# Four-layer graph kernel: layer 1's newest quarter last, weighing beside the scores, elu in PSUM, degrees in bfloat16 column tiles

## The chip, the cores and the metric

One core of one Trainium2 chip. The metric is the device time of one execution in microseconds (us). The kernel before took 1742.03 us (median of three runs, 1739.12 to 1742.09).

## What is computed

x has 8 batches of 2048 nodes with 64 features, adj is a 2048 x 2048 matrix of zeros and ones with a full diagonal, and H says which nodes belong to which of 64 hyperedges. Four layers follow each other, and each is `x = layernorm(x + layer(x))`. Cut to what the change touches:

```python
# layer 0: per node n and each hyperedge e that holds it
all_he = elu(beta[b,e,n] * h[b,n] + (1 - beta[b,e,n]) * agg[b,e])
g = sum_e coefs1[b,n,e] * all_he[b,e,n]
industry = (adj / deg) @ (x @ W_ind)          # deg = row sums of adj
c = softmax(attn_scores([industry, g]))       # tanh(f @ fcW + fcb) @ av
x = layernorm(x + c[0] * industry + c[1] * g)
# layer 1
dinv = rsqrt(row sums of (adj + I))
x = layernorm(x + (dinv * ((adj + I) @ (dinv * x))) @ W.T)
# layer 2: products with adj, apt = softmax(relu(emb @ emb.T)), node-wise weights, a bias
# layer 3: three steps of v = relu([v, adj @ v] @ W1.T + b1) @ W2.T + b2
```

## The kernel before, in words

adj (transposed) lies in SBUF for most of the kernel, in 16 row blocks of 128 and two column halves (`adj`, `adj_more`). The batches are handled as four pairs, so that 2 x 64 features fill 128 partitions or columns; the nodes as four quarters of 512, each of four tiles of 128. A product of adj with a pair takes float32r operands in two parts (high and low, `split`, L168), so each output quarter takes 2 x 16 matmuls of 128x512, and a pair 128 of them. The trace calls them `ug` (layer 0, `products`) and `u` (later layers). All matmuls go through `mm` (L172) and all transposes through `transpose` (L175); both keep the order of the program, which is thus the order of TensorE. `pin`, `hold` and `kept` are short names for the same fixing on other engines. What isn't fixed is put in order by a scheduler that goes by readiness and the program's order.

Stages, with their times in the profile: a start (h, the sums of agg, the nodes' rows gathered by hyperedge), to about 62 us. The **attention** of layer 0, to about 222 us: 16 node tiles, sorted so that the first has 12 steps and the last 1 or 2, 57 steps in all. In a step three matmuls put h and agg of one hyperedge slot into a PSUM tile `pz` (a ring of three, shared with small transposes), VectorE multiplies by the ratio `R` (L793), ScalarE takes exp (L795), VectorE makes elu by max and min (L797, into SBUF as `y`) and weighs it by `co` (L800 for a tile's first step, L802 for the others), and GpSimd adds it to `acc` (L803). At a tile's end GpSimd stores `acc` by an indirect DMA (L805). At a tile's first step `begin` prepares the next tile: GpSimd's gather, the split of its rows, sixteen-column matmuls `ps`, and four small VectorE instructions for `R` and `co` (L761 to L767). `slots` (L288 to L300) prepares the one-hot matrices of the tile after next, mostly on ScalarE.

**Mixing** of layer 0 and **layer 1** run together, to about 512 us. Mixing has 16 steps, one per pair and quarter: `mix_ind` (product with W_ind, scaling by the degree), `mix_g` (load and transpose of g), `mix_scores` (four tanh), `mix_weigh` (`pd`, a sigmoid as tanh, L937), `mix_end` (transposes `pt`, sum, layernorm, store to x1 in HBM). What TensorE does between them comes from a filler: a generator that gives one matmul of 128x512 at a time, first the rest of layer 0's products, then layer 1. `fill(n)` takes n of them. `tick`, `after` and `later` count filler matmuls and start other work when so many have gone by, so delays are written in matmuls. In attention, too, `fill(5)` and `fill(3)` are taken at each step, 345 in all. When layer 1 needs a part of x1 that isn't there, its generator answers "wait" and no matmul is put in.

The degrees come from 64 matmuls of float32r with a matrix of ones (`du`, in `degrees`), taken from the same filler between the first pair's two halves; `inverses` then makes 1/degree and dinv on VectorE and GpSimd.

Layer 1 takes each pair's parts from x1 (`l1_parts`), scales and splits them, makes its products in two halves of 128 x 512 x 2 columns, and `l1_end` multiplies by W, adds and normalizes. After mixing, `make_el` prepares the embeddings of layer 2 (`pb`, the bias), and `load_xn` loads pairs 0 to 2 of layer 1's result back, on ScalarE's DMA queue. Then apt (first score product `s` at 512.5 us), layer 2 and layer 3 follow.

Of the kernel before, what the change touches and what calls it, by code (L numbers as in the profile page):

```python
# [56 lines left out]
def tile_gnn_fast(  # L57
# [164 lines left out]
    ones_r = hy.tile([P, P], F32R, name="ones_r")  # L222
    nc.vector.tensor_copy(ones_r, ones)
# [118 lines left out]
    def products():  # L342
# [3 lines left out]
        def degrees(g):  # L346
            du = pph.tile([P, 2, C], F32, tag="ph", name=f"du{g}", bufs=2)
            for t in range(NT):
                for i in range(2):
                    mm(  # L350
                        du[:, i, :], lhsT=ones_r, rhs=adj_c(t, 2 * g + i), start=t == 0, stop=t == NT - 1
                    )
                    yield
            for i in range(2):
                c = 2 * g + i
                r = slice(c * P // NCH, (c + 1) * P // NCH)
                evacuate(deg4[r, :], du[r, i, :])

        def inverses():

            pdc = places["small"]([P, JT, P], "pdc")
            for j in range(JT):
                transpose(pdc[:, j, :], deg4[:, cols(j, P)])
            pdc = pdc.rearrange("p j (c r) -> p c j r", c=NCH)[:, :, :, 0]
            d1 = deg1.rearrange("p (c j) -> p c j", c=NCH)
            nc.vector.tensor_scalar(d1, pdc, 1.0, None, op0=ALU.add)
            nc.gpsimd.tensor_tensor(dinv, deg1, neg_half[:, :NT], ALU.pow)
            nc.vector.tensor_scalar(d1, pdc, 1.0, None, op0=ALU.max)
            nc.vector.reciprocal(deg1, deg1)
            for _ in range(20):  # L370
                yield
            for c in range(NCH):
                pt = places["small"]([P, C], "pinv")
                for j in range(JT):
                    k = c * JT + j
                    transpose(pt[:, cols(j, P)], deg1[:, k:k + 1].to_broadcast([P, P]))
                row = va.tile([P, C], F32, tag="ut", name="inv", bufs=2)
                nc.scalar.copy(row, pt)
                nc.sync.dma_start(inv_hbm[:, cols(c)], row)
                for _ in range(4):  # L380
                    yield

        for p in range(NP):
            for g in range(2):
# [3 lines left out]
                turning = inverses() if p == 0 and g == 1 else iter(())  # L388
                for t in range(NT):
                    for i in range(2):  # L390
                        for c in own:
                            mm(
                                u[c], lhsT=part[t // JT][i][:, t % JT, :], rhs=adj_c(t, c),
                                start=t == 0 and i == 0, stop=t == NT - 1 and i == 1,
                            )
                            tick()
                            if t > 1:
                                next(turning, None)
                            yield
                    if p == NP - 1 and g == 1 and t % JT == JT - 1:  # L400
                        first_parts(t // JT, free)
                    if p + 1 < NP and t % JT == JT - 1:
                        c = t // JT
                        if g == 1:
                            parts(p + 1, c)
                        if g == 1 and c < 2 or g == 0 and c >= 2:
                            fetch(p + 1, (c + 2) % NCH)
# [8 lines left out]
                if p == 0 and g == 0:  # L416
                    yield from degrees(0)
                    yield from degrees(1)
# [323 lines left out]
    with ExitStack() as pb_scope:  # L742
# [3 lines left out]

        def begin(t):
# [9 lines left out]
            for s, o in enumerate(ohs):  # L757
# [3 lines left out]
            nc.vector.tensor_tensor(  # L761
                R[:, 0:S], ps[:, 0:S, 0, :], hrow[:, None, BF:BF + 8].to_broadcast([P, S, B]), ALU.add
            )
            nc.vector.tensor_reduce(R[:, S], ps[:, 0:S, 1, :].rearrange("p s b -> p b s"), AX.X, ALU.add)
            nc.vector.reciprocal(R[:, 0:S + 1], R[:, 0:S + 1])
            co = pl.tile([P, 12, B], F32, tag="co", name="co", bufs=2)
            nc.vector.tensor_tensor(  # L767
                co[:, 0:S], ps[:, 0:S, 1, :], R[:, S:S + 1, :].to_broadcast([P, S, B]), ALU.mult
            )
            return S, both, ohs, R, co  # L770
# [3 lines left out]
        now = begin(0)  # L774
        slots(tiles[1], pps, "mm", 3)
        for k, t in enumerate(tiles):
            S, both, ohs, R, co = now
            acc = pl.tile([P, B, F], F32, tag="acc", name="acc", bufs=2)
            for s in range(S):
# [13 lines left out]
                nc.vector.tensor_tensor(z, z, R[:, s, :, None].to_broadcast([P, B, F]), ALU.mult)  # L793
                y = pl.tile([P, B, F], F32, tag="y", name="y", bufs=3)
                nc.scalar.activation(y, z, AF.Exp, bias=-1.0)  # L795

                nc.vector.scalar_tensor_tensor(y, z, 1.0, y, op0=ALU.max, op1=ALU.min)  # L797
                cb = co[:, s, :, None].to_broadcast([P, B, F])
                if s == 0:
                    nc.vector.tensor_tensor(acc, y, cb, ALU.mult)  # L800
                else:
                    nc.vector.tensor_tensor(y, y, cb, ALU.mult)  # L802
                    nc.gpsimd.tensor_tensor(acc, acc, y, ALU.add)  # L803

            nc.gpsimd.indirect_dma_start(  # L805
                out=gs_hbm[:], out_offset=bass.IndirectOffsetOnAxis(ap=order[:, t:t + 1], axis=0),
                in_=acc.rearrange("p b f -> p (b f)"), in_offset=None,
            )
# [97 lines left out]
    def mix_scores(i):  # L906
# [17 lines left out]
        after(5, differences)  # L924
        r, gn = rs[i], gns.pop(i)
# [37 lines left out]
    def l1_parts(p, c):  # L963
# [4 lines left out]
        y = staged("y")  # L968
        nc.sync.dma_start(y, x1_hbm[p][:, wide(c), :])

        def scale():
            pin(nc.gpsimd.tensor_tensor(y, y, dinv[:, wide(c), None].to_broadcast([P, JT, P]), ALU.mult))

        def cast():
            part[p, c] = split(va, y, f"v{c}", 1, [P, JT, P], pin=True)

        after(16, scale, 6, cast)

    def l1_load(p, c):
        x1 = staged("x1")  # L980
        nc.sync.dma_start(x1, x1_hbm[p][:, wide(c), :])
        return x1

    def l1_end(p, c, ut, x1):
# [5 lines left out]
        def add_up():  # L990
            pin(nc.vector.tensor_tensor(r, po, dinv[:, wide(c), None].to_broadcast([P, JT, P]), ALU.mult))
            pin(nc.gpsimd.tensor_tensor(r, r, x1, ALU.add))

# [7 lines left out]
        after(4, add_up, 6, *normalized(lp, r, dst, True, end))  # L1001
# [10 lines left out]
    def layer1(p):  # L1012

        for g in range(2):
            own = (2 * g, 2 * g + 1)
            ug = None
            for t in range(NT):
                while (p, t // JT) not in part:
                    yield "wait"
                if ug is None:  # L1020
                    ug = pph.tile([P, 2, C], F32, tag="ph", name="u1", bufs=2)
                    u = {c: ug[:, c % 2, :] for c in own}
                for i in range(2):
                    for c in own:
                        mm(
                            u[c], lhsT=part[p, t // JT][i][:, t % JT, :], rhs=adj_c(t, c),
                            start=t == 0 and i == 0, stop=t == NT - 1 and i == 1,
                        )
                        tick()
                        yield  # L1030
                if g == 1 and p + 1 < NP and t % JT == JT - 1:
                    l1_parts(p + 1, t // JT)
            for k, c in enumerate(own):
                ut = va.tile([P, C], F32, tag="ut", name="ut", bufs=2)
                pin(nc.scalar.copy(ut, u[c]))
                later(6 + 8 * k, lambda p=p, c=c, ut=ut, x1=l1_load(p, c): l1_end(p, c, ut, x1))
# [18 lines left out]
    for i in range(steps + 1):  # L1055
        k = 9 if i > NCH else 8
        if i < steps:
            mix_scores(i)
            fill(k)
        if i > 0:  # L1060
            mix_end(i - 1)
            fill(k)
        if i + 1 < steps:
# [3 lines left out]
            fill(k)  # L1067
        if i < steps:
            mix_weigh(i)
# [49 lines left out]
    fill(32)  # L1119
    for c in range(NCH):  # L1120
        make_el(c)
        fill(16)
        if c == 1:

            room.append(True)
            load_xn()
    norms = staged("emb").rearrange("p t f -> p (t f)")[:, 0:NT * D].rearrange("p (t d) -> p t d", d=D)
    nc.sync.dma_start(norms, emb.rearrange("(t p) d -> p t d", p=P))
    nc.vector.tensor_tensor(norms, norms, norms, ALU.mult)
    nrm = ap_.tile([P, NT], F32, name="nrm")  # L1130
    nc.vector.tensor_reduce(nrm, norms, AX.X, ALU.add)
    nc.vector.tensor_reduce(wrong[:, 5:6], nrm, AX.X, ALU.max)
    nc.vector.tensor_scalar(wrong[:, 5:6], wrong[:, 5:6], SUM_LIMIT, None, op0=ALU.is_gt)
# [590 lines left out]
    def check():  # L1724
        t, k = checks.pop(0)
        ar = va.tile([P, C], F32R, tag="ut", name="ar", bufs=2)
        nc.scalar.copy(ar, seen_a)  # L1727
        nc.vector.scalar_tensor_tensor(  # L1728
            ar.bitcast(F32), seen_a, 1.0, ar.bitcast(F32), op0=ALU.mult, op1=ALU.not_equal,
            accum_out=left[:, t, k:k + 1],  # L1730
# [892 lines left out]
```

## Time and profile before

| what | value |
|---|---|
| median of three runs | 1742.03 us (1739.12 to 1742.09) |
| profiled execution | 1745.85 us |
| its span | 1743.7 us |
| mean granted TensorE clock | 0.984 |
| busy: PE, DVE, ACT, POOL | 95%, 48%, 34%, 33% of the span |
| last exponential of attention starts | 221.4 us |
| last `pt` of mixing starts | 460.2 us |
| first `pb` starts | 481.2 us |
| first `s` of layer 2 starts | 512.5 us |

How it is read: a page gives for each engine the busy time in the span, and for groups of equal instructions the source line, the tiles that they write and read, their number, their busy time in us, the mean duration of one in ns, and the idle time of the engine ahead of them with what ended it. PE is TensorE's matmuls, PEld its weight loads, DVE VectorE, ACT ScalarE, POOL GpSimd, SP the queue that issues most transfers. In a list of waits, "A x L1 <- B y L2: 11.1, 12, 2.5" says that engine A sat idle ahead of line L1 for 11.1 us in 12 times, the longest 2.5 us, until engine B had done line L2. A table by stages gives for each stretch of time its length and each engine's busy time with the number of instructions.

### The profile page before, as it was taken

The numbers are of one execution on the slowest core, as the hardware profiler recorded it, in microseconds if no ns is written. First come the engines' busy times: TensorE is split into PE (matmuls) and PEld (weight loads), VectorE is DVE, ScalarE is ACT, GpSimd is POOL, SyncE is SP. The second block draws the span as 40 slices with busy tenths as digits, with TensorE's granted clock in tenths as the row PEclk, the third lists the DMA queues.
The fourth block names the chain that finished last, engine by engine and source line by source line (L and its number), as shares of the span: only waits on it lengthen the run. The fifth ranks groups of instructions, "written<-read, shape, count | busy, mean of one in ns | idle before, by whom it ended". The sixth has DMA issues, their size and how long they took to land.

```text
span 1743.7 us, 27994 instructions
## 1 busy us (share of the span) xinstructions
PE 1660.8 (95%) x11196; PEld 1209.8 (69%) x11196; DVE 832.2 (48%) x1547; ACT 589.5 (34%) x1031; POOL 571.8 (33%) x515
## 2 busy tenths in 40 slices
PE   6888899999899999999999999999989999999996
PEld 4667666666674444478788878888767877878775
DVE  7688845778642221210136147777523433433332
ACT  1345533444222212111213267878512222212221
POOL 4578845556534443422023001313210200202001
PEclk9999999999999999999999999999999999999998
DMA  9833334444330000027344457675571121211211
GB/s 342 277 126 124 125 122 136 142 145 146 112 121 6 30 27 5 24 71 293 112 133 138 117 137 154 138 168 123 152 260 43 49 61 43 61 48 42 57 42 39
DMA packets 171180, 195.83 MB, mean 112 GB/s; under 512 B 71536, under 2 KB 116336, under 8 KB 169760
## 3 DMA queue, kind: packets, MB, share of 16 engines
q1 hardware_dynamic: 160096, 154.54, 30.4%
q0 software_dynamic: 8544, 30.68, 5.2%
q10 hardware_dynamic: 2400, 8.72, 1.4%
q8 instruction: 90, 1.47, 0.4%
q14 instruction: 50, 0.41, 0.1%
HBM read 126.72 MB, written 67.17 MB: 111 GB/s over the span
## 4 chain that ended last, share of the span: by engine, by line
PE 78%; DVE 4%; DMA 3%; POOL 2%; issue 2%; ACT 1%; SPq 1%; POOLq 0%; ACTq 0%; DVEq 0%
PE u L172 39%; PE ua L172 13%; PE py L172 8%; PE pw L172 6%; PE ug L172 3%; PE pr L172 2%; PE po L172 1%; PE pf L172 1%; PE pt L175 1%; PE s L172 1%; PE pd L172 1%; PE pi L172 1%; PE pz L172 1%; POOL ln_r L862 0%; DMA adj_more<-adj_hbm 0%
## 5 line engine op out<-in xcount | busy, mean ns | idle before, releaser
L172 PE MATMUL ua<-pt,xn 128*128 128x512 f32 x512 | 230.2, 592 | 1.4 <-DVE pt L1150 1.4
L172 PEld LDWEIGHTS ua<-pt,xn 128*128 128x128 f32 x512 | 96.9, 190 | 111.1 <-issue 104.0
L1514 DVE COPY w_half<-pw 128x512 f32<-128x512 f32 x160 | 109.7, 705 | 91.1 <-PE pw L172 90.2
L1510 ACT COPY w_half<-pw 128x1024 f32<-128x1024 f32 x128 | 130.0, 1015 | 61.6 <-PE pw L172 61.5
L172 PE MATMUL py<-w_half,xg 128*32 128x128 f32 x4096 | 144.2, 281 | 3.2 <-issue 3.2
L172 PE MATMUL u<-adj,v0h 128*128 128x512 f32 x384 | 134.4, 427 | 1.1 <-ACT h L1818 1.1
L172 PEld LDWEIGHTS py<-w_half,xg 128*32 128x32 f32 x4096 | 112.5, 138 | 21.3 <-issue 4.6
L172 PE MATMUL u<-adj_more,v2h 128*128 128x512 f32 x384 | 126.5, 408 | 0.0
L172 PE MATMUL u<-adj_more,v2l 128*128 128x512 f32 x384 | 124.6, 401 | 0.0
L172 PE MATMUL u<-adj,v0l 128*128 128x512 f32 x384 | 124.5, 402 | 0.0
L172 PE MATMUL pw<-est,wst 64*128 64x256 f32 x1024 | 110.8, 320 | 0.8 <-ACT w_half L1510 0.4
L1156 POOL TENSOR_TENSOR acc<-acc,pt 128x512 f32<-128x512 f32 x60 | 76.5, 1276 | 104.2 <-DVE pt L1150 103.5
L1150 DVE TENSOR_SCALAR pt<-pt 128x512 f32<-128x512 f32 x64 | 29.8, 465 | 152.4 <-ACT pt L1149 152.3
L172 PEld LDWEIGHTS pw<-est,wst 64*128 64x128 f32 x1024 | 82.7, 187 | 26.3 <-ACT w_half L1510 16.7
L1727 ACT CAST ar<-fcav 128x512 fp32r<-128x512 f32 x64 | 39.5, 618 | 169.2 <-DMA fcav<-in_adj_t 164.5
L172 PE MATMUL u<-adj_more,v3l 128*128 128x512 f32 x288 | 93.8, 401 | 2.0 <-DVE v3l L168 2.0
L1728 DVE SCALAR_TENSOR_TENSOR ar<-fcav,ar 128x512 f32<-128x512 f32 x64 | 45.2, 707 | 102.9 <-ACT ar L1727 102.9
L172 PE MATMUL u<-adj,v1h 128*128 128x512 f32 x288 | 93.7, 403 | 0.0
L1149 ACT ACTIVATE pt<-s 128x512 f32<-128x512 f32 x64 | 38.0, 598 | 164.4 <-PE s L172 164.4
L172 PE MATMUL u<-adj_more,v3h 128*128 128x512 f32 x288 | 93.6, 403 | 0.0
L1699 POOL TENSOR_TENSOR x<-x,rows 128x512 f32<-128x512 f32 x16 | 22.6, 1433 | 212.0 <-PE pt L175 127.7
L172 PE MATMUL u<-adj,v1l 128*128 128x512 f32 x288 | 92.0, 397 | 0.0
(406 smaller groups left out, 3273.2 us busy)
## 6 DMA issues: line engine op xcount, KB each, us to landing
fcav<-in_adj_t SPq DMA_DIRECT2D x64, 256.0 KB, 2.9
u_hbm<-ut SPq DMA_DIRECT2D x48, 256.0 KB, 2.8
xg<-u_hbm SPq DMA_DIRECT2D x24, 512.0 KB, 7.1
adj<-in_adj_t POOLq DMA_DIRECT2D x16, 512.0 KB, 7.7
adj_more<-in_adj_t POOLq DMA_DIRECT2D x16, 512.0 KB, 7.4
adj_hbm<-adj_more SPq DMA_DIRECT2D x16, 512.0 KB, 6.1
x_hbm<-r SPq DMA_DIRECT2D x28, 256.0 KB, 2.4
hs_hbm<-st ACTq DMA_DIRECT2D x8, 584.0 KB, 5.9
```

The source lines that it names most:

```text
L172: tc.keep_in_program_order(nc.tensor.matmul(*args, **kw))
L175: tc.keep_in_program_order(nc.tensor.transpose(dst, src, ident))
L1149: nc.scalar.activation(pt, s, AF.Exp)
L1150: nc.vector.tensor_scalar(pt, pt, 1.0, None, op0=ALU.max)
L1156: nc.gpsimd.tensor_tensor(accs[c], accs[c], pt, ALU.add)
L1510: pin(nc.scalar.copy(dst, pw.rearrange("p j o n -> p n (j o)")))
L1514: pin(copy(dst[:, :, 2 * j:2 * j + 2], bank.rearrange("p o n -> p n o")))
L1699: nc.gpsimd.tensor_tensor(xs, xs, b2.to_broadcast([P, JT, P]), ALU.add)
L1727: nc.scalar.copy(ar, seen_a)
L1728: nc.vector.scalar_tensor_tensor(ar.bitcast(F32), seen_a, 1.0, ar.bitcast(F32), op0=ALU.mult, op1=ALU.not_equal, accum_out=left[:, t, k:k ...
```

## The change

- *Degrees.* The upper halves of adj's float32 words are read as bfloat16 (adj holds only zeros and ones), with a stride of two. 64 matmuls of 128x32 by 128x512 in four column tiles sum one quarter each; they come in four bursts of 16 inside the second half of pair 0's product (at row blocks 5, 9, 13, 15) and are not taken as filler slots. One copy takes the result out. `inverses` runs in the next pair's first half, with longer distances.
- *Attention.* elu is written back into PSUM, and the weighing reads it there. It is issued one step later: mult(s), weigh(s-1), elu(s), in this fixed order. The four ratio instructions for the next tile follow the first elu of the tile. The exponential gets its own tile in `y`'s ring of three.
- *Mixing.* `mix_weigh` and `mix_end` of a step move into the next step's round: weigh beside the next scores, the end one fill later. The sum of x and g moves from the scores to `mix_sum`. Fills are 11 or 12, three a round, instead of 8 or 9, four a round.
- *Layer 1.* Both halves of a pair are begun before its newest quarter is needed; the quarters that a half takes are 0, 1, 2 and later 3, the other 0, 1 and later 2, 3. Staging tiles are given out through a queue (`ask`, `serve`, `left`).
- *After mixing.* `load_xn` comes ahead of `fill(40)` (before: after the second `make_el`, which followed `fill(32)`), the distances of `make_el` are 12 instead of 16, and the check of the embeddings' norms goes through the queue.
- *Layer 3.* The check of the input compares a bfloat16 copy.

```diff
-        def degrees(g):
-            du = pph.tile([P, 2, C], F32, tag="ph", name=f"du{g}", bufs=2)
-            for t in range(NT):
-                for i in range(2):
-                    mm(
-                        du[:, i, :], lhsT=ones_r, rhs=adj_c(t, 2 * g + i), start=t == 0, stop=t == NT - 1
-                    )
-                    yield
...
+        def degrees(du, q):
+            for t in range(q * JT, (q + 1) * JT):
+                for c in range(NCH):
+                    r = slice(c * P // NCH, (c + 1) * P // NCH)
+                    top = adj_c(t, c).bitcast(BF16).rearrange("p (n h) -> p n h", h=2)[:, :, 1]
+                    mm(du[r, 0, :], lhsT=ones_h[:, r], rhs=top, start=t == 0, stop=t == NT - 1)
+            if q == NCH - 1:
+                nc.scalar.copy(deg4, du[:, 0, :])
...
                 for t in range(NT):
+                    if counted and t in (5, 9, 13, 15):
+                        degrees(du, (5, 9, 13, 15).index(t))
...
-                if p == 0 and g == 0:
-                    yield from degrees(0)
-                    yield from degrees(1)
...
+        def weighed(acc, z, cb, first, t):
+            if first:
+                hold(nc.vector.tensor_tensor(acc, z, cb, ALU.mult))
+            else:
+                y = pl.tile([P, B, F], F32, tag="y", name="y", bufs=3)
+                hold(nc.vector.tensor_tensor(y, z, cb, ALU.mult))
+                nc.gpsimd.tensor_tensor(acc, acc, y, ALU.add)
...
-                nc.vector.tensor_tensor(z, z, R[:, s, :, None].to_broadcast([P, B, F]), ALU.mult)
-                y = pl.tile([P, B, F], F32, tag="y", name="y", bufs=3)
-                nc.scalar.activation(y, z, AF.Exp, bias=-1.0)
-
-                nc.vector.scalar_tensor_tensor(y, z, 1.0, y, op0=ALU.max, op1=ALU.min)
+                hold(nc.vector.tensor_tensor(z, z, R[:, s, :, None].to_broadcast([P, B, F]), ALU.mult))
+                e = pl.tile([P, B, F], F32, tag="y", name="e", bufs=3)
+                nc.scalar.activation(e, z, AF.Exp, bias=-1.0)
+                if rest:
+                    rest.pop()()
+
+                hold(nc.vector.scalar_tensor_tensor(z, z, 1.0, e, op0=ALU.max, op1=ALU.min))
+                if s == 0 and k + 1 < NT:
+                    now[-1]()
                 cb = co[:, s, :, None].to_broadcast([P, B, F])
...
+                rest.append(lambda z=z, acc=acc, cb=cb, s=s, t=t, S=S: weighed(
+                    acc, z, cb, s == 0, t if s == S - 1 else None
+                ))
...
     for i in range(steps + 1):
-        k = 9 if i > NCH else 8
+        k = 12 if i > NCH else 11
+        if i > 0:
+            mix_weigh(i - 1)
         if i < steps:
             mix_scores(i)
-            fill(k)
-        if i > 0:
-            mix_end(i - 1)
             fill(k)
         if i + 1 < steps:
             mix_load(i + 2)
             mix_ind(i + 1)
             mix_g(i + 1)
-            fill(k)
         if i < steps:
-            mix_weigh(i)
+            mix_sum(i)
+        fill(k)
+        if i > 0:
+            mix_end(i - 1)
             fill(k)
...
-        for g in range(2):
+        u, held = {}, [None, None]
+        for g, quarters in ((0, (0, 1, 2)), (1, (0, 1)), (0, (3,)), (1, (2, 3))):
...
-        after(16, scale, 6, cast)
+            after(16, scale, 12, cast)
+
+        ask(begin)
+    def serve():
+        while asked and (taken[0] < 2 or taken[0] - 2 in free_again):
+            taken[0] += 1
+            asked.pop(0)(taken[0] - 1)
...
-    fill(32)
+    room.append(True)
+    load_xn()
+    fill(40)
     for c in range(NCH):
         make_el(c)
-        fill(16)
-        if c == 1:
-
-            room.append(True)
-            load_xn()
+        fill(12)
...
-        nc.scalar.copy(ar, seen_a)
+        short = ar.bitcast(BF16)[:, 0:C]
+        nc.scalar.copy(short, seen_a)
```

## The prediction

> **What bounds the kernel now.** The page's first rows say that TensorE is busy 95% of the span and that 78% of the chain that ended last is PE. So a change pays only if TensorE has fewer instructions, sits idle for less, or runs at a higher clock. I cut the part that the diff touches into four stages: attention to the last exponential (221.4), mixing to the last transpose of an answer (460.2), then to the first bias product `pb` (481.2), then to the first score product `s` of layer 2 (512.5).
>
> ```profile
> core 0: us, PE busy (x) PEld busy (x) DVE busy (x) ACT busy (x) POOL busy (x), PEclk, DMA share, GB/s
> 62.00:221.40 159.40, 140.21 (x590) 107.11 (x591) 133.29 (x248) 81.68 (x214) 130.80 (x112) 0.95 0.48 162
> 221.40:460.20 238.80, 231.76 (x1028) 151.68 (x1026) 158.32 (x218) 91.68 (x158) 131.44 (x104) 1.00 0.42 135
> 460.20:481.20 21.00, 15.66 (x70) 12.69 (x71) 12.75 (x23) 4.76 (x9) 10.41 (x8) 0.92 0.46 158
> 481.20:512.50 31.30, 31.27 (x141) 25.41 (x142) 14.78 (x31) 6.38 (x13) 8.13 (x5) 0.89 0.50 153
> ```
>
> TensorE idles 19.2 + 7.0 + 5.3 + 0.0 = 31.5 us here, and the lower clock costs about 8.0 + 0 + 1.7 + 3.4 = 13 us. That is the ceiling for rearranging. The waits name the idle time, first attention's and then that of the later stages:
>
> ```profile
> DVE pz L793 <- PE pz L172: 11.1, 12, 2.5
> POOL acc L803 <- DVE y L802: 11.0, 12, 1.7
> PE pz L172 <- DVE y L797: 8.2, 12, 1.5
> DVE y L797 <- ACT y L795: 6.5, 7, 2.4
> DVE deg L368 <- POOL dinv L367: 4.7, 1, 4.7
> ```
> ```profile
> PE pb L172 <- DMA xn<-x_hbm: 5.4, 1, 5.4
> PE pt L175 <- DVE ind L937: 3.6, 1, 3.6
> ```
>
> In attention everybody waits for everybody: PE, DVE and POOL are busy 140, 133 and 131 of 159 us. After it TensorE runs nearly without a gap, and the two gaps that matter lie at the end, each followed by matmuls at 0.43 us instead of 0.2335 (in the timeline, a pair of products starts 0.47 us after the last one, after the gaps 0.85).
>
> **What the skill says here.** The Trainium skill, page "SBUF — State Buffer", section "Who interferes with whom": a VectorE instruction with both inputs in SBUF takes its second one through an interface that GpSimd's reads also need, and one has to wait for the other; with at most one SBUF input there is no conflict. The trace of before fits:
>
> ```profile
> L797 DVE SCALAR_TENSOR_TENSOR y<-pz,y x55: 618/680/693, 67.5 to 219.0; 128x512 f32<-128x512 f32 x55
> L802 DVE TENSOR_TENSOR y<-y,co x40: 675/692/3433, 74.3 to 218.1; 128x512 f32<-128x512 f32 x40
> L800 DVE TENSOR_TENSOR acc<-y,co x15: 665/858/2373, 68.4 to 219.6; 128x512 f32<-128x512 f32 x15
> ```
>
> (Columns: shortest, middle, longest in ns.) The max/min L797 has one operand in PSUM and never exceeds 693; the weighing, with both in SBUF, reaches 3433. I go by both.
>
> The skill's "TensorE: Matmul & The Clock Gate", "Part 3: Packing small matmuls", says that matmuls narrower than the array run side by side in their own column strips, and gives 2.38 times for three. The nearest row is `pd`: two strips, four passes in 1.01 us (start to next start), where the full-width `pi` takes 0.86 us for two passes, so 1.7 times. No row shows four strips.
>
> **The change part by part.**
>
> *Degrees.* Removed: 64 float32r matmuls, 64 x 0.2335 = 14.9 us of TensorE, all in attention (86.8 to 115.9), and two evacuations. Added: 64 bfloat16 matmuls in four bursts of 16. With no overlap they cost the same 14.9; at the 1.7 of `pd` 8.8; I take the page's 2.38, 6.2 us. The bursts are no slots of the filler, so the attention stage keeps its 345 slots, all of which are now products: 64 products move forward out of the later stages. By the order of instructions of both programs: products to the last transpose 600 before, 577 after; from there to `pb` 50 and 42; from `pb` to `s` 94 and 60. 65 x 0.2335 = 15.2 us leave the later stages. The transfers of adj's second half are issued from 71 to 91.5 us and land 7.4 us later, while its product begins at about 86 and uses a row block each 2 us or more; no wait is counted. The inverses move one product later; POOL's 2.95 us power no longer stops DVE (4.7 us).
>
> *Attention, DVE.* The weighing reads PSUM. Stretch removed, over the whole trace: L802 38.1 - 41 x 0.685, L800 16.4 - 16 x 0.685, together 15.4 us. Added: the order is fixed as mult(s), weigh(s-1), elu(s), and elu(s) needs exp(s). A mult is done 0.68 after its start, exp starts 0.04 later and takes 0.60, so elu starts 1.37 after mult, where two DVE instructions back to back take 1.20: 0.17 x 57 = 9.7 us. This replaces the 6.5 us of the same wait now: +3.2. ACT's slots are next: in the new order a group for the tile after next (three slots: 162.67 to 164.85, 2.2 us) stands ahead of one exponential in each of 14 tiles, and behind it waits elu, behind that all of DVE, then POOL's adding and TensorE's `pz`. DVE has 0.6 us of cover: at most 14 x 1.6 = 22 us, at least 0 where ACT ran ahead; DVE's own work is about 126 us (57 x 1.97, 16 ratios of 0.7, some casts), so there are over 20 us of slack to catch up in. I take 3.4.
>
> Sum for attention: -15.4 - 4.7 + 3.2 + 3.4 + 6.2 (bursts; the 64 slots stay) = **-7.3**. Limits: TensorE's own work is 345 + 171 matmuls x 0.2335 = 120.5, small ones about 6, bursts 6, cold clock 5: 138; POOL's 131. So the stage can't lose more than about 20.
>
> *Mixing.* 23 fewer products (-5.4), eight more `po` rows of `ut` by `bd_w` (one per finished quarter, 8 x 0.21 = +1.7), and the last `pt` has a further fill before it: the 3.6 us gap goes. Answers reach memory about 0.4 iteration (5 us) later, and layer 1 asks for parts of them; the newest quarter is now used last, and the order of instructions shows only 16 empty slots. I add 1 for stalls and lower clock: **-6.3**.
>
> *To pb.* Only 42 x 0.2335 = 9.8 us of work is left to lay beside a chain of layernorm (460.2 to the store at 471.3), its answer, and the embeddings (issued 474.5, used 481.2). TensorE idles longer, about 10 us, but the chain sets the time: 21.0 now; the layernorm starts the same, fewer instructions compete, up to 3 MB of xn go ahead on ACT's queue instead of 1 MB behind. **-1.5** (from -4 to +2).
>
> *pb to s.* 34 products fewer, 7.9 us; the cold start remains: **-7.5**.
>
> *Rest.* Layer 3's check in bfloat16: 64 x (0.62 ACT + 0.71 DVE) lies beside layer 3's products, which wait for neither (u rows: 0.0 to 2.0 idle); 0, and if ACT needed longer there is the idle 164 us in front of L1727. SP's queue gets the same transfers in other places; norms leave the tail, 0.
>
> Sum -7.3 - 6.3 - 1.5 - 7.5 = -22.6. The profiled execution took 1745.85 (span 1743.7 and 2.1 around it), so 1723.2 on its own terms; the median of the runs is 3.8 lower, 1742.03, and I state the forecast against that: **1719.4 us**.
>
> **Rivals.**
> 1. *Attention reaches TensorE's limit* of 138: -20 instead of -7.3, so 1742.0 - 20 - 15.3 = 1706.7. For it: all three busy engines lose work or waits. Against: 16 tile changes with their chain gather, split, ratios. 0.15.
> 2. *The strips don't overlap or need a load each*: 14.9 instead of 6.2 (+8.7): 1728.1. For it: 64 weight loads, and the moving operand is read with a stride. Against: `pd`. 0.10.
> 3. *The tail is bound by transfers*: the products that leave it were only cover; `pb` 3 later instead of 1.5 earlier and of the 7.5 only 3 remain: 4.5 + 4.5 more, 1728.4. 0.12.
> 4. *Slower: the fixed DVE order.* A z stays in its PSUM buffer until weigh, one DVE instruction and one step longer, in a ring of three that slots also use; with the slot groups ahead of exp every tile stops DVE for the whole 2.2 us, and with it PE. Price: 14 x 2.2 = 30.8 + 9.7, bursts 6.2, less the 4.7 and half of the stretch (7.7): +34.3 in attention, against -15.3 behind it: 1761.0. It decides from the point where attention is over 15.3 us longer, that is 0.27 us a step. For it: DVE was free to fill such waits until now and isn't any more. Against: the 20 us of slack. 0.15.
>
> **Numbers.** The forecast 0.48, its own range 1711 to 1732. About 0.2% (3.5 us) is what a measurement of this kernel can tell from no change. Faster: 0.48 + 0.15 + 0.10 + 0.12, less 0.07 for mixtures that eat the gain, 0.78; same 0.07; slower 0.15. The range takes in rivals 1 to 3 and the nearer half of 4: 1702 to 1746.
>
> **What would show it.** Bursts: 16 matmuls within 1.6 us each (right) or 3.7 (rival 2). Weighing never over 0.70 us. DVE's wait for exp about 10 to 15 us in many small pieces; in pieces of 2 us, 14 times, it is rival 4. Last exponential near 214. Last `pt` near 447, no wait ahead of it; `pb` near 466, `s` near 490. Wrong would be: adj's second half late for the first pair, a wait of TensorE for parts in mixing of more than 3 us, or layer 2 and 3 (512.5 to the end, 1231 us) changed by over 2 us.

## The result: slower by 1.4%

The changed kernel takes 1767.97 us (median of six runs, 1762.97 to 1771.23), the kernel before 1741.62 in the runs beside it. The ratio is 1.0142, 95% interval 1.0126 to 1.0158. Forecast was 1719.4, with a range of 1702 to 1746 and a chance of 0.15 for slower. The profiled execution took 1768.42 (span 1766.6), against 1745.85 (1743.7) before.

### The profile after

The same four stages, cut at the same events (62 us, last exponential, last `pt`, first `pb`, first `s`), and below them mixing in the kernel before:

```profile
core 0: us, PE busy (x) PEld busy (x) DVE busy (x) ACT busy (x) POOL busy (x), PEclk, DMA share, GB/s
62.00:225.40 163.40, 148.09 (x690) 110.69 (x689) 123.31 (x254) 87.64 (x226) 128.46 (x119) 0.98 0.50 169
225.40:492.40 267.00, 240.06 (x1009) 156.02 (x1008) 155.53 (x222) 91.78 (x156) 133.08 (x103) 0.93 0.37 118
492.40:518.40 26.00, 11.63 (x45) 8.77 (x43) 13.54 (x24) 4.27 (x7) 9.00 (x7) 0.74 0.57 214
518.40:539.00 20.60, 20.60 (x109) 16.95 (x109) 9.16 (x18) 5.69 (x11) 3.63 (x3) 1.00 0.27 82
```
```profile
222.10:460.60 238.50, 231.46 (x1028) 151.51 (x1027) 157.68 (x217) 91.04 (x157) 131.63 (x103) 1.00 0.42 135
```

The second line holds most of the loss. Mixing runs 19 matmul instructions fewer (1009 against 1028) and is 28.5 us longer. TensorE idles there for 26.9 us instead of 7.0, and its busy time is 8.6 us more although it does less, because the granted clock is 0.93 and no longer 1.00; 19.9 + 8.6 = 28.5. In the list of waits from 222 us to 540, TensorE's first two lines are new; the kernel before has no wait of `u` at all there:

```profile
PE u L172 <- ACT v2h L167: 28.4, 4, 14.4
PE u L172 <- ACT v1h L167: 4.6, 1, 4.6
PE pg L175 <- DMA gn<-gs_hbm: 4.1, 1, 4.1
```

`v2h` is the high part of the third quarter of a pair of layer 1, cast on ScalarE. Of its 28.4 us, 14.0 lie in mixing; the longest stop, 14.4, comes just behind the last `pt` and so falls in the third line of the table. The timeline of TensorE shows one stop in mixing (start, length, instructions; the bracket holds the idle time), and below it a `pd` of the kernel before:

```profile
366.72 0.60 PE L175 MATMUL pt<-ident,ind 128*128 128x128 f32 x4
373.46 1.22 PE L172 MATMUL u<-adj_more,v2h 128*128 128x512 f32 x2 [6.15 <-ACT v2h L167]
374.62 1.98 PE L172 MATMUL pd<-t,fcav 128*64 128x512 f32 x4
376.52 2.02 PE L172 MATMUL pf<-ind,fcav 64*128 64x512 f32 x4
378.37 1.02 PE L172 MATMUL pf<-gt,fcav 64*128 64x512 f32 x4
```
```profile
309.29 1.08 PE L172 MATMUL pd<-t,fcav 128*64 128x512 f32 x4
```

Mixing's own `pd` and `pf` stand behind the waiting matmul, so the stop hits mixing too, and with it the next part. The same four `pd` took 1.08 us in the kernel before and take 1.98 here: behind this stop TensorE works at about half the rate. Two more stops look like this (6.21 us at 440.6, 14.37 at 508.4).

SyncE's queue shows where such a part comes from. In the kernel before, the load of quarter 0 of pair 1 was issued 22.6 us after the store of its data (316.37); in the changed one 2.6 us after.

```profile
316.37 0.32 SPq L948 DMA_DIRECT2D x_hbm<-r  x1
324.99 0.32 SPq L948 DMA_DIRECT2D x_hbm<-r  x1
338.97 0.32 SPq L969 DMA_DIRECT2D y<-x_hbm  x1
```
```profile
331.48 0.32 SPq L973 DMA_DIRECT2D x_hbm<-r  x1
334.04 0.38 SPq L995 DMA_DIRECT2D y<-x_hbm  x1
```

Over all 16 parts the time from store to load has a median of 5.7 us before, with 10 of 16 over 3.5 us; after, 2.7 us, none over 3.5. Layer 1 used to have a stock of stored quarters; now it takes each as it comes. From the store to the first matmul that reads it, the part at 373.46 needed 10.7 us (store 362.76, load 365.63, scaling 371.73, cast 372.79), and TensorE stood still for the end of it.

This distance, from the issue of a quarter's store on SyncE to the start of the first matmul that reads it, is the stock itself. Over the 16 quarters of a timeline its median is 32.2 us in the kernel before, never under 11.8, and 15.0 in the changed one.

Stage by stage, spans of the two profiled executions (attention from the first to the last exponential; in the kernel before the last one starts at 222.1 and the last of the `pt` at 460.6, a little behind the 221.4 and 460.2 at which the prediction cut):

| stage | before | after | difference | forecast |
|---|---|---|---|---|
| start, to the first exponential | 66.9 | 71.3 | +4.4 | 0 |
| attention | 155.2 | 154.1 | -1.1 | -7.3 |
| mixing, to the last `pt` | 238.5 | 267.0 | **+28.5** | -6.3 |
| to the first `pb` | 20.6 | 26.0 | +5.4 | -1.5 |
| to the first `s` | 31.3 | 20.6 | -10.7 | -7.5 |
| layers 2 and 3 | 1231.2 | 1227.6 | -3.6 | 0 |

### The profile page after: what moved, and what is told of

Read it like the earlier page. It is cut to its first block, busy times and chain, and to the rows that moved or that the text cites. A ratio compares the mean times of both kernels' runs of the same rounds, so it can differ in the third digit from the quotient of the medians.

```text
span 1766.6 us, 27957 instructions
## 1 busy us (share of the span) xinstructions
PE 1658.9 (94%) x11196; PEld 1204.2 (68%) x11196; DVE 819.2 (46%) x1545; ACT 591.2 (33%) x1030; POOL 563.6 (32%) x515
## 4 chain that ended last, share of the span: by engine, by line
PE 83%; DMA 5%; DVE 4%; ACT 2%; POOL 2%; issue 2%; SPq 1%; ACTq 0%; POOLq 0%; DVEq 0%
PE u L172 39%; PE ua L172 12%; PE py L172 7%; PE pw L172 6%; PE ug L172 5%; PE pr L172 2%; PE pz L172 2%; PE pf L172 2%; PE po L172 1%; DMA r<-in_x_n 1%; PE pt L175 1%; PE s L172 1%; DMA x_hbm<-r 1%; PE pd L172 1%; PE pi L172 1%
## 5 line engine op out<-in xcount | busy, mean ns | idle before, releaser
L172 PE MATMUL u<-adj_more,v2h 128*128 128x512 f32 x384 | 127.7, 413 | 28.4 <-ACT v2h L167 28.4
L172 PEld LDWEIGHTS u<-adj_more,v2h 128*128 128x128 f32 x384 | 71.9, 193 | 46.1 <-ACT v2h L167 30.2
L1798 ACT CAST ar<-fcav 128x512 bf16<-128x512 f32 x64 | 39.5, 617 | 167.1 <-DMA fcav<-in_adj_t 166.2
L1799 DVE SCALAR_TENSOR_TENSOR ar<-fcav,ar 128x512 bf16<-128x512 f32 x64 | 46.5, 727 | 100.5 <-ACT ar L1798 100.4
```

What stands on the lines that cost most here:

```text
L172: tc.keep_in_program_order(nc.tensor.matmul(*args, **kw))
L1798: nc.scalar.copy(short, seen_a)
L1799: nc.vector.scalar_tensor_tensor(short, seen_a, 1.0, short, op0=ALU.mult, op1=ALU.not_equal, accum_out=left[:, t, k:k + 1],)
```

## The experiments

Three theories were set against each other at first. **A**: GpSimd's `r + gn` waits for a load of x whose buffer comes back a round later, and everything behind it on GpSimd is late. **B**: layer 1's new order or its staging queue makes the parts late. **C**: the 64 slots that the degrees gave up were filled with products, so layer 1 stands 64 matmuls nearer to mixing, and the distance is used up. Later expectations name a fourth, **D**: the distance is enough, and mixing's rounds are slow for a chain of their own. A had GpSimd's longest wait on its side: it waits 57.1 us for `r<-in_x_n` from 222 to 500 us.

### Theory A: a third buffer

```diff
-            rs[i] = mp.tile([P, JT, P], F32, tag="r", name="r", bufs=2)
+            rs[i] = mp.tile([P, JT, P], F32, tag="r", name="r", bufs=3)
...
-            mix_x(i + 2)
+            mix_x(i + 3)
...
+    mix_x(2)
```

> The changed kernel with one edit: mixing's sum tile r has three buffers instead of two, and the load of x is issued three steps ahead instead of two. Theory A (GpSimd's r+gn waits for a load of x whose buffer the step before last gives back one round later than it used to, and the layernorm's power and layer 1's scaling stand behind it): GpSimd's wait for that load goes from 57 us to under 15, the stage from the last exponential to the last pt from 267 us to 235 to 248, the time to 1735 to 1750. Theory B (layer 1's new order or its staging queue makes the parts late) and theory C (the filler is 64 products further on, so layer 1 catches up with mixing): the stage stays within 6 us of 267 and the time within 6 us of 1768.

1773.1 us (1771.44 to 1774.6), ratio 1.0179 [1.0162, 1.0196] to the kernel before. The wait for x is gone, but GpSimd's waits from 222 to 500 us now begin so:

```profile
POOL y L998 <- DMA y<-x_hbm: 75.4, 11, 9.3
POOL ln_r L885 <- DVE ln_e L884: 21.9, 14, 9.1
```

The wait moved to the scaling of layer 1's part, whose load follows mixing's store. Mixing took 273.5 us, 0.5 more than theories B and C allowed. Theory A is false: GpSimd's long wait was a sign of the shortage, not its cause.

### Undoing one part at a time

Each of these is the changed kernel with one part of the change's diff reversed. Mixing's loop:

```diff
-        k = 12 if i > NCH else 11
-        if i > 0:
-            mix_weigh(i - 1)
+        k = 9 if i > NCH else 8
         if i < steps:
             mix_scores(i)
             fill(k)
+        if i > 0:
+            mix_end(i - 1)
+            fill(k)
...
```

> The changed kernel with mixing's loop as before (sum beside the scores, end one fill after the scores, weighing in its own round, four fills of 8 or 9). Theory A: the stage returns to 235 to 245 us and the time to 1735 to 1748. Theory B: no return, over 1760. Theory C: no full return, TensorE still waits over 10 us for parts of layer 1, 1750 to 1765.

1754.62 us, ratio 1.0079 [1.0059, 1.01]; mixing 251.1, and TensorE still waits 28.5 us for `v2h` (16.6 of them once, at the end). Half of the loss is back. As theory C has it; theory A's figure of 235 to 245 is missed. The same kernel was run once more, under a label that wrongly names a fill of four:

> The changed kernel with mixing's loop as before, at five filler matmuls a step: a second look at the trace of old_mixing. Theory C: waits for parts of about 28 us as in the first, 1748 to 1758.

1754.13 us (one run), mixing 251.1, waits for `v2h` 28.8.

The degrees, as slots of the filler again:

```diff
-                    if counted and t in (5, 9, 13, 15):
-                        degrees(du, (5, 9, 13, 15).index(t))
...
+                if p == 0 and g == 0:
+                    yield from degrees(0)
+                    yield from degrees(1)
```

> The changed kernel with the degrees and inverses as before (64 float32r matmuls taken as filler slots). Theory A: mixing's stage keeps its 13.5 us rounds, 260 us or more, the time is 1762 to 1778. Theory C: with 64 products fewer in attention layer 1 doesn't catch up, the stage falls below 250 us and the time to below 1755. The bursts' own cost is read from attention: it is shorter by 0 to 6 us here.

1756.48 us, ratio 1.0088 [1.0072, 1.0105]; mixing 249.0, 18 us shorter than in the changed kernel, and the wait for `v2h` falls from 28.4 to 6.3. Theory A had asked for 260 or more. The stated limits of theory C (mixing below 250, time below 1755) are met for the stage and missed by 1.5 us for the time. Attention was *longer* here, 161.8, not shorter: VectorE waits 26.8 us for exp instead of 18.0. Why is not shown.

Layer 1 in its old order:

```diff
-        for g, quarters in ((0, (0, 1, 2)), (1, (0, 1)), (0, (3,)), (1, (2, 3))):
+        for g in range(2):
...
-            after(16, scale, 12, cast)
+        after(16, scale, 6, cast)
...
-    fill(40)
+    fill(32)
```

> The changed kernel with layer 1 and what comes after mixing as before (each half takes its four quarters in turn, staging without a queue, cast after 6 matmuls, xn loaded after the second make_el). Theory B: TensorE's waits for parts in mixing fall from 19 us to under 8 and the time by over 10 us. Theory A: the rounds stay at 13.5 us, and since the newest quarter is needed earlier TensorE waits longer: 1768 to 1785.

1799.0 us, ratio 1.0331 [1.0314, 1.0349]; mixing 298.4. Theory B is false (and A's 1785 at most is missed too), and layer 1's new order and queue with the new tail are together worth about 31 us once the stock is gone: with the old order TensorE waits 23.1 us for the newest quarter and 12.8 for the third.

The elementwise part of attention:

```diff
-                hold(nc.vector.scalar_tensor_tensor(z, z, 1.0, e, op0=ALU.max, op1=ALU.min))
+                nc.vector.scalar_tensor_tensor(y, z, 1.0, y, op0=ALU.max, op1=ALU.min)
...
+                    nc.vector.tensor_tensor(y, y, cb, ALU.mult)
+                    nc.gpsimd.tensor_tensor(acc, acc, y, ALU.add)
```

> The changed kernel with attention's elementwise part as before (elu into SBUF, the weighing right behind it from SBUF, the scheduler's own order), the degrees still in bursts. The stock of products ahead of mixing is the same, so mixing keeps its waits and its 267 us within 6. Attention shows what the new elementwise part is worth: by the prediction's terms 8.8 us (15.4 less 3.2 and 3.4), so 163 us instead of 154 and 1773 to 1782 in all; if the stretched weighing lay off the path, 154 to 157 us and 1765 to 1772.

1773.11 us, ratio 1.0169 [1.0152, 1.0186]; attention 157.8 against 154.1, mixing 263.4. The new elementwise part is worth 3.7 us in its stage, close to what was expected if the stretched weighing lay off the path (up to 157) and far from the 163 of the prediction's terms; the time is 1.1 us above the first case's range.

### Theory C: the stock alone

First the other way round: the kernel *before*, only further ahead.

```diff
-                fill(5)
+                fill(6)
```

> The kernel before, with six filler matmuls a step in attention instead of five: 57 products more are done ahead of mixing, nothing else. Theory C: TensorE now waits for parts in mixing (over 10 us, from 0), each stop followed by the low clock, and the time is 1748 to 1770 though no work was added; attention is longer by 5 to 13 us, mixing by 0 to 20 instead of shorter by 13. Theory D: mixing is shorter by the 13 us that attention is longer, 1736 to 1748.

1761.9 us (1761.44 to 1762.37), ratio 1.011 [1.0093, 1.0127]. No work was added and nothing else was changed, and TensorE has the new waits (226 to 540 us):

```profile
PE u L172 <- ACT v3h L167: 16.4, 3, 6.4
PE u L172 <- ACT v2h L167: 7.3, 2, 4.6
PE po L172 <- ACT ut L1035: 4.2, 2, 2.1
```

Attention grew by 7.0 us and mixing, instead of losing the 57 matmuls (13.3 us), grew by 17.3. That is theory C by itself, and theory D's 1736 to 1748 is missed. Then the changed kernel, set back:

```diff
-                fill(5)
+                fill(4)
```

> The changed kernel, with four filler matmuls a step in attention instead of five: 57 products stay behind for mixing, so layer 1 follows mixing at a greater distance. Theory C (the 64 slots that the degrees no longer take have used up that distance, and TensorE now waits for parts that mixing has only just stored): TensorE's waits for parts fall from 34 us (226 to 540) to under 14, mixing's stage from 267 to 240 to 252 us, the time to 1735 to 1757; a part is loaded later than 3 us after its store for over half of the 16. Theory D (the distance is enough, the rounds are slow for a chain of their own): waits and time within 6 us of the changed kernel's.

1739.22 us (1736.71 to 1743.72, 20 runs), ratio 0.9979 [0.9971, 0.9988]: one digit takes off about 29 us. Attention 145.9, mixing 248.0; one wait for a part is left, 12.0 us at the very end. One expectation failed: the loads still follow the stores after 2.6 us (median). With the new order and queue a part is asked for long before it is used, so this interval doesn't measure the stock in these kernels. The same holds for the 2.7 us of the changed kernel. The time from the store to the first matmul does measure it: its median went from 15.0 to 22.5 us.

```diff
-        k = 12 if i > NCH else 11
+        k = 10
```

> The changed kernel, with three fills of 10 a round of mixing instead of 11 or 12: about 90 filler matmuls fewer in the 16 rounds, 30 a round where layer 1 gains 32 with each stored quarter, so the distance grows instead of shrinking. Theory C: waits for parts under 12 us, mixing's stage 225 to 245, and the 90 products lie beside the last layernorm and the loads behind it: 1722 to 1748. Theory D: the rounds stay at 15 us and more: 1760 to 1775.

1752.7 us, ratio 1.0063 [1.0046, 1.008], missing the expectation by 5 us. The waits for parts fell as foreseen (5.2 us), but others took their place: `po` for ScalarE's copy (11.7, new), `pf` (6.2 and 5.7, against 0.5 and 3.0 in the changed kernel) and `pg` (6.1 against 4.1). That the rounds now have too little cover for their own chain is the likely reading; no run here takes it apart. Giving the stock back in attention costs less of this (`pf` 4.9 and 1.2).

The same with the third buffer of r:

```diff
-        k = 12 if i > NCH else 11
+        k = 10
...
-            rs[i] = mp.tile([P, JT, P], F32, tag="r", name="r", bufs=2)
+            rs[i] = mp.tile([P, JT, P], F32, tag="r", name="r", bufs=3)
```

> As the last, and r with three buffers and its load three steps ahead. With fewer matmuls a round GpSimd's wait for x can become the limit: if it does, this is faster than with the ring of two by 5 to 15 us; if it doesn't, within 4 us of it.

1756.89 us, ratio 1.0085 [1.0068, 1.0102]: 4.2 us slower than with two buffers, so x isn't the limit here either.

### Versions that beat both

> The changed kernel with mixing's loop as before and four filler matmuls a step in attention: answers are stored half a round earlier and 57 products stay for mixing, so both things that had used up layer 1's distance are undone. Theory C: waits for parts under 8 us ahead of the last quarter, mixing's stage 236 to 246, attention 146: 1722 to 1738, faster than before.

The edits are `fill(4)` and mixing's loop of the kernel before:

```diff
-                fill(5)
+                fill(4)
...
-        k = 12 if i > NCH else 11
-        if i > 0:
-            mix_weigh(i - 1)
+        k = 9 if i > NCH else 8
...
         if i < steps:
-            mix_sum(i)
-        fill(k)
-        if i > 0:
-            mix_end(i - 1)
+            mix_weigh(i)
             fill(k)
```

**1722.62 us** (1721.65 to 1724.81), ratio 0.9879 [0.9862, 0.9896]. Mixing is 1.5 us below the expected 236, attention 144.3 instead of 146. Its stages, in the columns of the first table:

```profile
62.00:212.90 150.90, 132.37 (x616) 96.62 (x615) 123.19 (x253) 84.17 (x219) 123.84 (x115) 0.98 0.53 176
212.90:447.40 234.50, 230.08 (x1018) 151.08 (x1017) 145.10 (x212) 90.64 (x157) 127.84 (x101) 0.99 0.41 134
447.40:469.60 22.20, 17.82 (x78) 13.48 (x76) 12.89 (x25) 3.51 (x7) 10.61 (x7) 0.92 0.58 208
469.60:496.30 26.70, 25.32 (x127) 19.95 (x128) 15.54 (x27) 7.31 (x15) 8.69 (x6) 1.00 0.42 133
```

In mixing TensorE idles 4.4 us at a clock of 0.99, and 1.8 us of waiting for `v2h` is all that is left in 226 to 540 us, beside 0.9 for `v3l` and 0.5 for `v3h`. Against the changed kernel with `fill(4)`, the old loop is 13.5 us shorter in mixing with 32 matmul instructions fewer (7.5 us), and gives 1.1 us back behind it. So the new loop of mixing, meant as a gain, is a loss with this stock too: its stage holds 7.2 us more of busy TensorE and 6.3 more of idle time.

Mixing's loop, layer 1 and the tail as before, with `fill(4)`:

```diff
-                fill(5)
+                fill(4)
...
-    room.append(True)
-    load_xn()
-    fill(40)
+    fill(32)
```

> The changed degrees and attention with four filler matmuls a step, and mixing, layer 1 and what follows as in the kernel before (layer 3's check new). Layer 1 stands within 8 products of where it stood before. Theory C: no wait for parts, mixing 236 to 244, then 21 and 31 as before, attention 146: 1728 to 1740.

1728.81 us, ratio 0.9915 [0.9898, 0.9931]: attention 143.9, mixing 236.6. So the new degrees and attention alone, with the stock about as before, gain 0.85%; layer 1's new order and the new tail add the last 6 us. The kernel before with four fills a step was not run, so whether it too would gain from another count is open.

The stock in the main runs, beside TensorE's waits for parts of layer 1 in 226 to 540 us:

| run | store to first matmul, median of 16 | waits for parts | mixing | time |
|---|---|---|---|---|
| before | 32.2 | 0 | 238.5 | 1741.62 |
| before_fill6 | 15.9 | 23.7 | 255.8 | 1761.9 |
| after | 15.0 | 33.8 | 267.0 | 1767.97 |
| old_mixing | 17.0 | 30.0 | 251.1 | 1754.62 |
| old_layer1 | 12.7 | 35.9 (41.0 to 570 us) | 298.4 | 1799.0 |
| old_degrees | 27.5 | 6.3 | 249.0 | 1756.48 |
| attention_fill4 | 22.5 | 12.0 | 248.0 | 1739.22 |
| front_only_fill4 | 28.8 | 0 | 236.6 | 1728.81 |
| mixing_old_fill4 | 30.6 | 3.2 | 234.5 | 1722.62 |

## Why the prediction was wrong

**The failed step** is the one for mixing: "Answers reach memory about 0.4 iteration (5 us) later ... and the order of instructions shows only 16 empty slots. I add 1 for stalls and lower clock". With the other terms kept, the 1 us came out as about 36 (28.5 + 5.4 - 1.7 + 3.6). The order of instructions says where the program leaves slots empty, not whether the data are there when a slot that is filled comes up. The step before it fed the error: 64 products moving forward were counted as 15.2 us off the later stages. They do move, but each brings layer 1 nearer to mixing, and layer 1 can't pass it. Had I followed the parts through the trace of before (store, load, scaling, cast, first use) I would have read the stock there: 32.2 us from store to first matmul in the median. The 64 matmuls at 0.2335 are 15 us of it, and mixing's new loop takes more (22.5 against 30.6 between attention_fill4 and mixing_old_fill4). What is left, 15.0 us, is little more than the hand-over itself, which took 9.5 to 11.0 us wherever TensorE waited for a part in mixing. Both halves were tested: with one of the two undone, `fill(4)` takes off about 29 us and mixing's old loop 13; with both, 45.

**None of the rivals** was this. Rival 4 ended on the right side for the wrong reason: attention was not longer. The fixed order of VectorE did cost 18.0 us of waiting for exp in 18 pieces of up to 1.7 us, more than the 10 to 15 foreseen, and not in 14 pieces of 2. My list of what would be wrong did name "a wait of TensorE for parts in mixing of more than 3 us"; I had given it no price.

**The degrees** were right in kind and too dear in size: 6.2 us forecast. The timeline of a burst:

```profile
97.40 0.40 PE L172 MATMUL ug<-adj,v1l 128*128 128x512 f32 x1
97.73 1.09 PE L172 MATMUL du<-adj,ones_h 128*32 128x512 bf16 x16
98.75 0.73 PE L172 MATMUL ug<-adj,v1h 128*128 128x512 f32 x2
```

Sixteen in 1.02 us to the next matmul's start; four bursts 4.1 us. Rival 2 is refuted.

**The stretch** was removed, as the Trainium skill's page "SBUF — State Buffer", section "Who interferes with whom", has it for at most one operand in SBUF. No weighing takes over 692 ns now, where one took 3433 before:

```profile
L793 DVE TENSOR_TENSOR y<-pz,co x41: 678/683/692, 77.0 to 226.7; 128x512 f32<-128x512 f32 x41
L790 DVE TENSOR_TENSOR acc<-pz,co x16: 679/680/682, 75.1 to 225.2; 128x512 f32<-128x512 f32 x16
```

Its worth was mis-sized: 8.8 us net by my terms, 3.7 measured (old_attention). VectorE's work in the stage is 17.2 us less than there (118.0 against 135.2), but two waits eat most of it:

```profile
DVE pz L824 <- ACT e L820: 18.0, 18, 1.7
DVE y L793 <- POOL acc L794: 10.1, 12, 1.9
```

The wait for exp is 10.8 us in old_attention. The second wait isn't there at all: the exponential's tile and the weighing's now share `y`'s ring of three, so VectorE waits for GpSimd's addition to give a buffer back. The prediction has no term for it, and a larger ring was not tried. With the old elementwise part the new degrees make attention 2.6 us longer than before (157.8 against 155.2), where I had +1.5 (6.2 less 4.7). So 2.6 - 3.7 = -1.1 is the stage's account. The two parts aren't additive: the new elementwise part with the old degrees takes 161.8.

**To pb and s**: together -5.3 where -9.0 was forecast. TensorE idles 14.4 of the 26.0 us to `pb`, and all of it is the stop for `v2h` that ends at 508.44. About 4.1 us of this stop come from the change itself. GpSimd has scaled the part at 503.65, but ScalarE casts it only after three issues of xn, which `load_xn` now puts ahead of the cast in its queue:

```profile
502.62 1.03 POOL L998 TENSOR_TENSOR y<-y,dinv 128x512 f32<-128x512 f32 x1
506.42 1.31 ACTq L1067 DMA_DIRECT2D xn<-x_hbm  x3
507.77 0.62 ACT L167 CAST v2h<-y 128x512 fp32r<-128x512 f32 x1 [8.95 <-issue]
```

For the other 15 parts of this run the cast starts within 1.8 us of the scaling's end. The prediction had counted the earlier xn as a gain. No run has the early load taken out alone, so the 4.1 is read from the trace and not tested. The embeddings land 11.6 us (median) after their issue instead of 6.8, beside 3 MB of xn instead of 2, so rival 3 was right that the transfers get longer; but `pb` starts without a gap behind the products ahead of it, so its price isn't what is seen. From `pb` to `s`, 32 fewer matmul instructions (109 against 141, 7.5 us) and a clock of 1.00 instead of 0.89 give the 10.7.

**The start** is 4.4 us later in this profile. The change need not be the cause: over the profiled executions of all kernels here the first exponential starts anywhere from 66.3 to 71.8 us, the latest in before_fill6, whose start is the unchanged one. What makes it vary was not tried. **Layer 3's check** shows no cost, as forecast; why layers 2 and 3 are 1.5 to 7 us shorter in all variants stays open. One with the old check is among them (before_fill6, 1226.3).

## What to carry to other kernels

When two streams share an in-order engine and one consumes what the other produces, work that fills idle slots early is not free: it eats the stock between them. Below the time of the hand-over (here about 10 us) both streams stop together, and the loss can be larger than the work moved: 57 matmuls of 13.3 us brought forward made the kernel before 19 us slower. Before moving filler forward, measure in the trace how far behind its producer the consumer is at each hand-over, and count the matmuls moved against it. A fill count that was tuned for the old stock has to be set again after any edit that changes the work outside the slots: here one digit separates 1768 from 1739 us.

## What the runs showed of the hardware

- Four column strips of 32 overlap better than I had dared to take from three: 16 matmuls of 512 columns in 1.02 us where one after the other at 0.2335 would be 3.7, a factor of 3.6. The Trainium skill's page "TensorE: Matmul & The Clock Gate", Part 3, gives 2.38 for three strips, the trace of before 1.7 for two. These matmuls read bfloat16 with a stride of two elements; no run has them without the stride.
- Six stops of 1.7 to 6.2 us and some shorter ones, 26.9 us in all, go with a granted clock of 0.93 in a stage of 267 us, and with 8.6 us more of busy time for fewer matmuls. Against the stage of before, 19.9 us more of idle time made it 28.5 us longer, 1.4 times as much.
- A stop of 1.69 us (310.77 to 312.46, behind one of 0.46 at 309.2) is followed by the low clock as well. From 313.5 us on the clock shown is half for 3.4 us, and 9 matmuls fall into them where 16 fall into the 3.4 us that follow:

```profile
310.10:313.50 3.40, 1.71 (x5) 0.60 (x4) 1.26 (x3) 2.31 (x5) 3.40 (x4) 1.00 0.26 77
313.50:316.90 3.40, 3.40 (x9) 2.64 (x8) 3.12 (x4) 0.00 (x0) 0.77 (x1) 0.50 0.00 0
316.90:320.30 3.40, 3.40 (x16) 2.45 (x15) 0.69 (x1) 0.60 (x1) 0.00 (x0) 1.00 0.59 193
```
